# Gated recurrence and binary FFN on one core: the mix difference in another buffer, a step's tanh ahead of a copy, gating in the x tile, and one form for the last rounds

## The chip, the cores and the metric

The kernel runs on one core of one Trainium2 chip. The metric is the device time of one execution in microseconds, lower is better. The time before is 449.11 us, the median of three runs (447.16 to 449.99). A core has five engines with an instruction queue each: PE multiplies matrices, ACT applies functions element by element, DVE and POOL do vector arithmetic, SP issues most DMAs. Each engine works through its queue in order, and semaphores hold an instruction until its inputs are there. Times inside the kernel are from one profiled execution, counted from the start of its span.

## The reference

The input x is 2 sequences of 4096 rows with 256 numbers each.

```python
u = x @ W_in + b_in;  g = sigmoid(x @ W_gate + b_gate)
h_t = tanh(h_prev @ A + u_t @ Bm)              # along the sequence
y_t = g_t * (h_t @ C.T + u_t @ D.T) + (1.0 - g_t) * x_t
x = layernorm(x + (ys @ W_out + b_out + x))
h = gelu(x @ bw1.T + b1, exact)                # 1024 wide, bw = mean(|w|) * sign(w)
x = layernorm(x + (h @ bw2.T + b2))
```

So there are a recurrence with a gate and a residual, a layer norm, a feed-forward layer whose weights are signs with a scale per row, and a second layer norm.

## The kernel before, in words

**Recurrence.** Each sequence is cut into 64 segments of 64 positions; 128 segments advance side by side. A step (`steps`, L157 and L158) is one product of the state tile `st` on PE and one tanh on ACT; each needs the tanh before it. There are 48 warm-up steps that give each segment its start state, and then 64. `compare` and `count` count whether the start states agree with the end states, and a slow path at the end of the kernel, not taken here, redoes the work if they don't.

**Chunks.** The rows are worked on in 16 chunks of 512. For one chunk:

- `gates` (L313) multiplies x by the gate weights on PE, and a tanh on ACT (L365) writes the gate tile `tg`. Early in the kernel this work is cut into pieces (`parts`) that fill PE between steps. Their tanh is passed through `later`, which keeps one back, and the next step releases it.
- `mix` computes C h + D u on PE (L374, `ps_y`), adds the output bias to the chunk's rows `xn` on POOL (L359), and forms the difference `d` to x on DVE (L381). `mix_end` gates it with two DVE operations (L386 and L389), and y is the result.
- `project` multiplies y by W_out (L399, `ps_z`), and DVE adds the rows (L410). `stats1` collects the statistics, with an inverse root on POOL (L266); `shift` (L271, DVE) and `norm` (L279, ACT) apply them.
- The normed rows are then turned. For chunks 0, 1 and 15 `turn` does it on PE (L430). For the others (`far` in the loop) `blocks` transposes 32x32 blocks on DVE (L449), sixteen DMAs on SP's queue put them in place (L455), `split_hi` copies the result to a rounded high part on ACT (L463), and `split_lo` forms the rest on DVE (L467). High and low parts are `xhi` and `xlo`.
- The feed-forward layer has four groups. `up(g)` multiplies by signs on PE (L486, `ps_h`), takes two gelus on ACT (L496) and a rounded high copy (L505). `low(g)` forms the rest on DVE (L512). `down(g)` multiplies both by the second signs (L528, `ps_o`). `down 3` ends with a scaling on DVE (L544, tile `o`).
- `add` (L550) adds the rows, `stats` collects statistics, `store` shifts and norms, on ACT or DVE, and issues the DMA to `out_y` on SP.

**Buffers.** Tiles with one tag share a fixed number of buffers, and an instruction that writes a tile waits until a buffer is free. `ps_h`, `ps_g`, `ps_u` and the product of `count` share three PSUM buffers; `ps_y`, `ps_z` (from chunk 2 on) and `ps_t` share one; `ps_o` has one. Gate tiles have nine, x tiles eight, `xhi` two, and `o` one, shared by the scaled output and by the mix difference.

**Order.** The order is written out by hand. The order in which the Python code calls pieces is the order of each engine's queue. `emit` and `do` add up a cost for pieces and put a step in when a pace is reached; `step()` puts one in directly while any are left. A round c of the main loop (c from 0 to 14) works on `up` of chunk c, the end of chunk c-1, the turning of chunk c+1, and mix and projection of chunk c+2. After round 14 the rest of chunk 15 is written out. Before the loop, chunks 0 to 2 are mixed, projected and normed among the last pieces of gates. `load` gets a chunk's inputs and states (`hu`), `load_n` its rows (`xn`); both queue on SP. A step that completes chunk 0, 1 or 2 issues the load of its states.

Round 14 is written differently from the others before the change: chunk 13's `add` is on POOL, its `stats` stands after `low 2`, and its `store` is on DVE behind `down 1`.

Of the kernel before, what the change touches and what calls it, by code (L numbers as in the profile page):

```python
# [8 lines left out]
FP = mybir.dt.float32  # L9
# [7 lines left out]
P = 128  # L17
B, T, DM, S, H = 2, 4096, 256, 64, 1024
KD = DM // P
# [4 lines left out]
N = 512  # L24
# [3 lines left out]
TB = N // P  # L28
# [9 lines left out]
def gated_recurrence_then_binary_ffn(  # L38
# [16 lines left out]
    nc = tc.nc  # L55
# [227 lines left out]
    def all_stats(r, name):  # L283
# [2 lines left out]
            what(range(TB))  # L286
        return st

    waiting = None

    def later(what, *args):
        if waiting is None:
            what(*args)
        else:
            waiting.append((what, args))
            if len(waiting) > 1:
                what, args = waiting.pop(0)
                what(*args)

# [29 lines left out]
    class Chunk:  # L329


        def __init__(self, c, name, at=lambda a, c: a[c]):
            self.c, self.nm, self.at, self.xt = c, name, at, None
            self.far = False

        def load_x(self):
            self.xt = xp.tile([P, KD, N], FP, tag="xt", name=f"xt_{self.nm}", bufs=XTB)
# [31 lines left out]
        def mix(self):  # L369

            nm, xt_ = self.nm, self.xt
            ps = p_m.tile([P, KD, N], FP, tag="m", name=f"ps_y{nm}")
            for m in range(KD):
                nc.tensor.matmul(  # L374
                    ps[:, m, :], cd[:, bass.ts(m, P)], self.hu, start=True, stop=True
                )
                if m < KD - 1:
                    yield
            self.add_row(self.xn, bo_r)
            self.d = wk.tile([P, KD, N], FP, tag="o", name=f"d{nm}", bufs=1)  # L380
            nc.vector.tensor_sub(self.d, ps, xt_)  # L381
            yield

        def mix_end(self):
            d = self.d
            nc.vector.scalar_tensor_tensor(d, self.t, 1.0, d, ALU.add, ALU.mult)  # L386
            yield
            y = self.y = self.t
            nc.vector.scalar_tensor_tensor(y, self.xt, 2.0, d, ALU.mult, ALU.add)  # L389
            yield  # L390

# [251 lines left out]
    done = 0  # L643
# [6 lines left out]
    def next_steps():  # L650
        nonlocal done
        steps(plan[done])
        done += 1
        if done == WARM:
            first_states()
        for i in range(3):
            if done == WARM + (i + 1) * SPC:
                ch[i].load_h()
        for what, args in waiting or ():
            what(*args)  # L660
        if waiting:
            waiting.clear()

    def emit(what, pieces, pace=5600):
# [8 lines left out]
    def step():  # L673
        if ready():
            next_steps()
# [17 lines left out]
    def parts(n, pace):  # L693
        emit("part", (next(early, None) for _ in range(n)), pace)

    ET = mybir.EngineType
    with tc.manual_schedule(engines={ET.PE, ET.Activation, ET.DVE, ET.Pool, ET.SP}):
        waiting = []
        for c in range(FIRST + 1, FIRST + 6):
            load_xT(c)  # L700
        idle_products(7)
        emit("u", u_of_chunks(FIRST), 1 << 30)
        since = 0
        pairs = [(5, 6), (7, 8), (9, 10), (11, 12), (13, 14), (), (1, 2)]
        loads = [[10, 11], [12, 13], [14, 15, 0], [1, 2], [3], [], []]
        for n, pair in enumerate(pairs):
            before = 2 if n == 0 else 1
            parts(before, EARLY)
            if pair:
                emit("", u_of_chunks(*pair))  # L710
                if pair == (13, 14):
                    emit("", u_of_chunks(15, 0))
                emit("u", [None], EARLY)
            for c in loads[n]:
                load_xT(c)
            if n == 0:
                load_weights()
            if n == 3:
                halve_weights()
            if n >= 5:  # L720
                load_xT(n + 3)
                for i in ((0,), (1, 2))[n - 5]:
                    ch[i].load_n()
                    ch[i].load_u()
            for i in range(7 - before):
                if 1 <= n < 5 and i == 0:
                    load_w(n - 1)
                if 2 <= n < 6 and i == 3:
                    prepare_w(n - 2)
                parts(1 if (n, i) != (6, 5) else 0, EARLY)  # L730
        assert done >= WARM + SPC, done
        emit("u", u_of_chunks(3), EARLY)
        for i in range(4):
            ch[i].xt = x_tiles[i]
        do(0, "mix", pace=850)
        do(0, "mix_end")
        parts(2, 600)
        assert done >= WARM + 2 * SPC, done
        do(1, "mix", pace=850)
        do(1, "mix_end")  # L740
        parts(1, 600)
        do(0, "project", 0, p_2, "o", pace=1700)
        do(0, "project", 1, pace=1700)
        do(0, "stats1")
        assert done >= WARM + 3 * SPC, done
        do(2, "mix", pace=1700)
        do(0, "shift")
        do(1, "project", 0, p_2, "o", pace=1700)
        do(0, "norm")
        do(1, "project", 1, pace=1700)  # L750
        do(1, "stats1")
        mixed = ch[2].mix_end()
        next(mixed)
        parts(1, 1700)
        while waiting:
            next_steps()
        waiting = None
        do(0, "turn", True)
        emit("", mean_w2())
        do(1, "norm", nc.vector)  # L760
        do(0, "rest")
        next(mixed)
        parts(2, 1700)
        for i in (4, 5):
            do(i, "load_x")
        end = len(ch) - 1
        parts_met = compare()
        since = -1 << 40
        late = gates(ch[10:], TB)
        for c in range(end):  # L770
            far = 0 < c < end - 1
            if c > 0:
                do(c + 1, "shift")
                do(c + 1, "norm")
                do(c - 1, "low", 3)
                if far:
                    do(c + 1, "blocks")
            do(c, "up", 0)
            step()
            do(c - 1, "down", 2)  # L780
            if c == end - 2:
                do(c, "low", 0)
            if c > 0:
                do(c + 2, "mix")
                do(c + 2, "mix_end")
            if c != end - 2:
                do(c, "low", 0)
            if c == end - 1:
                next(parts_met)
                next(parts_met)  # L790
            do(c + 3, "load")
            do(c + 6, "load_x")
            if c % 2 == 0:
                do(10 + c // 2, "load_gate_x")
            do(c, "up", 1)
            step()
            do(c - 1, "down", 3)

            def add():
                do(c - 1, "add", range(TB), nc.gpsimd if c == end - 1 else nc.vector)  # L800
                if c < end - 1:
# [8 lines left out]
            if c == end - 1:  # L810
                next(parts_met)
                next(parts_met)
            if not 1 <= c <= 12:
                add()
            do(c + 1, "rest")
            do(c, "up", 2)
            if far:
                do(c + 1, "split_hi")
            do(c, "low", 2)
            if c < end - 1:  # L820
                do(c - 1, "store", range(TB), nc.scalar)
                do(c + 3, "load_n")
            if c == end - 1:
                do(c - 1, "stats")
            if c == end - 2:
                assert done == len(plan), done
# [94 lines left out]
```

## Time and profile before

| what | value |
|---|---|
| median of three runs | 449.11 us (447.16 to 449.99) |
| the profiled execution | 451.14 us |
| its span on the core | 449.4 us |
| mean granted PE clock | 0.994 |
| PE busy | 428.2 us, 95% of the span |
| DVE busy | 332.0 us, 74% |
| ACT busy | 284.4 us, 63% |
| POOL busy | 152.5 us, 34% |

A line of a group or a timeline names the start and duration in us, the engine, the line of the kernel, the operation, what it writes and reads (`out<-in`, shapes, number of instructions), and in brackets the idle time before it with what ended it. A window line gives the busy time and the number of instructions of PE, of PE's weight loads, of DVE, ACT and POOL, then the granted clock as a share of full speed, the DMA engines' share and GB/s. A wait line names the one that waited and the one waited for, with total us, number of times and the longest.

### The profile page before, as it was taken

The numbers are of one execution on the slowest core, as the hardware profiler recorded it, in microseconds if no ns is written. First come the engines' busy times: TensorE is split into PE (matmuls) and PEld (weight loads), VectorE is DVE, ScalarE is ACT, GpSimd is POOL, SyncE is SP. The second block draws the span as 40 slices with busy tenths as digits, with TensorE's granted clock in tenths as the row PEclk, the third lists the DMA queues.
The fourth block names the chain that finished last, engine by engine and source line by source line (L and its number), as shares of the span: only waits on it lengthen the run. The fifth ranks groups of instructions, "written<-read, shape, count | busy, mean of one in ns | idle before, by whom it ended". The sixth has DMA issues, their size and how long they took to land.

```text
span 449.4 us, 6825 instructions
## 1 busy us (share of the span) xinstructions
PE 428.2 (95%) x2402; PEld 344.2 (77%) x2402; DVE 332.0 (74%) x571; ACT 284.4 (63%) x476; POOL 152.5 (34%) x177
## 2 busy tenths in 40 slices
PE   8999998989999999999999999999999999898992
PEld 4665766678887879787878787878787878687882
DVE  0245946786878788887888797869797979795874
ACT  2443441575676666767676777767776776848571
POOL 1000510364042425252525343434343445352513
PEclk9999999999999999999999999999999999999997
DMA  8877523400151615162515242524242223210102
GB/s 292 293 281 257 196 82 123 160 1 0 41 171 42 216 39 175 34 190 68 154 53 185 75 136 69 188 72 141 69 144 69 78 86 86 85 44 28 47 1 99
DMA packets 31480, 51.34 MB, mean 114 GB/s; under 512 B 5329, under 2 KB 19665, under 8 KB 31441
## 3 DMA queue, kind: packets, MB, share of 16 engines
q1 hardware_dynamic: 30864, 50.48, 35.7%
q8 instruction: 21, 0.34, 0.3%
q10 hardware_dynamic: 576, 0.37, 0.3%
q14 instruction: 19, 0.15, 0.1%
HBM read 31.43 MB, written 8.39 MB: 89 GB/s over the span
## 4 chain that ended last, share of the span: by engine, by line
PE 61%; DVE 12%; SPq 9%; ACT 8%; DMA 4%; issue 3%; POOL 2%; POOLq 0%; DVEq 0%; ACTq 0%
PE ps_o L528 15%; PE ps_h L486 14%; PE ps_g L313 10%; SPq L455 9%; PE ps_z L399 8%; PE ps_s L157 5%; PE ps_y L374 5%; ACT xn L279 4%; PE ps_u L131 3%; DVE hlo L512 2%; DMA xt<-in_xT 2%; DMA hu<-st 1%; ACT h L496 1%; DMA xlo<-xb 1%; DVE bs_a L256 1%
## 5 line engine op out<-in xcount | busy, mean ns | idle before, releaser
L528 PE MATMUL ps_o<-sg,hhi 128*128 128x256 f32 x496 | 121.8, 286 | 2.1 <-DVE o L544 2.1
L528 PE MATMUL ps_o<-sg,hlo 128*128 128x256 f32 x496 | 118.3, 279 | 0.8 <-DVE hlo L512 0.8
L496 ACT ACTIVATE h<-ps_h,bias_c,al 128x512 f32<-128x512 f32 x128 | 95.7, 772 | 27.8 <-PE ps_h L486 23.5
L528 PEld LDWEIGHTS ps_o<-sg,hhi 128*128 128x128 f32 x496 | 93.6, 189 | 3.3 <-DVE o L544 2.6
L528 PEld LDWEIGHTS ps_o<-sg,hlo 128*128 128x128 f32 x496 | 93.5, 189 | 2.0 <-DVE hlo L512 1.2
L486 PE MATMUL ps_h<-xhi,sg 128*128 128x512 f32 x256 | 93.0, 444 | 1.4 <-ACT h L496 1.4
L512 DVE TENSOR_TENSOR hlo<-h,hhi 128x1024 fp32r<-128x1024 f32 (+1 forms) x65 | 78.4, 1224 | 6.5 <-ACT hhi L505 6.4
L486 PE MATMUL ps_h<-xlo,sg 128*128 128x512 f32 x256 | 80.1, 393 | 1.3 <-DVE xlo L440 1.2
L359 POOL TENSOR_TENSOR xn<-xn,bo_r 128x256 f32<-128x256 f32 x64 | 50.5, 820 | 82.8 <-DMA xn<-in_x 77.5
L266 POOL TENSOR_TENSOR rs_b<-rs_b,neg_half 128x4 f32<-128x4 f32 (+1 forms) x17 | 28.1, 1655 | 120.9 <-DVE rs_b L265 120.8
L505 ACT CAST hhi<-h 128x1024 fp32r<-128x1024 f32 (+1 forms) x65 | 67.4, 1038 | 2.0
L313 PE MATMUL ps_g<-xt,w_gate 128*128 128x384 f32 (+3 forms) x208 | 66.2, 430 | 0.1
L486 PEld LDWEIGHTS ps_h<-xhi,sg 128*128 128x128 f32 x256 | 46.5, 189 | 20.0 <-issue 11.7
L157 PEld LDWEIGHTS ps_s<-st,wab 128*128 128x128 f32 x224 | 37.9, 189 | 27.7 <-ACT st L158 16.0
L158 ACT ACTIVATE st<-ps_s 64x128 f32<-64x128 f32 x112 | 30.0, 268 | 45.7 <-PE ps_s L157 45.3
L399 PE MATMUL ps_z<-w_out,tg 128*128 128x256 f32 x256 | 58.2, 379 | 0.0
L486 PEld LDWEIGHTS ps_h<-xlo,sg 128*128 128x128 f32 x256 | 48.1, 188 | 12.8 <-DVE xlo L440 2.1
L359 POOL TENSOR_TENSOR xn<-xn,b_r 128x256 f32<-128x256 f32 x64 | 51.3, 831 | 2.0 <-PE ps_t L430 2.0
L399 PEld LDWEIGHTS ps_z<-w_out,tg 128*128 128x128 f32 x256 | 47.2, 190 | 5.7
L157 PE MATMUL ps_s<-st,wab 128*128 128x128 f32 x224 | 44.6, 281 | 3.7 <-ACT st L158 3.5
L266 POOL TENSOR_TENSOR rs_a<-rs_a,neg_half 128x4 f32<-128x4 f32 x16 | 17.2, 1076 | 72.5 <-DVE rs_a L265 69.3
L279 ACT ACTIVATE xn<-xn,nm_a,rs_a 128x256 f32<-128x256 f32 x60 | 31.2, 591 | 14.6 <-DVE nm_a L271 14.6
(76 smaller groups left out, 466.5 us busy)
## 6 DMA issues: line engine op xcount, KB each, us to landing
xt<-in_xT SPq DMA_DIRECT2D x35, 512.0 KB, 4.3
xn<-in_x SPq DMA_DIRECT2D x16, 512.0 KB, 3.3
out_y<-xn SPq DMA_DIRECT2D x15, 512.0 KB, 2.6
xlo<-xb SPq DMA_DIRECT2D x208, 32.0 KB, 1.9
hu<-st SPq DMA_DIRECT2D x32, 128.0 KB, 2.3
w1t<-in_w1T SPq DMA_DIRECT2D x2, 512.0 KB, 5.1
w1n<-in_w SPq DMA_DIRECT2D x2, 512.0 KB, 6.3
w2t<-in_w2T SPq DMA_DIRECT2D x2, 512.0 KB, 5.3
```

The lines of the kernel that those rows point to most:

```text
L157: nc.tensor.matmul(p_h, ab, st[:, j].rearrange("p b k -> p (b k)"), start=True, stop=True)
L266: nc.gpsimd.tensor_tensor(rs, rs, neg_half[:, cut], ALU.pow)
L279: nc.scalar.activation(r, r, AF.Identity, bias=self.sh[:, i : i + 1], scale=rs)
L313: nc.tensor.matmul(ps[:, cut], w_gate[:, k, bass.ts(m, P)], xt_[:, k, cut], start=k == 0 and i == 0, stop=k == KD - 1, skip_group_check=True,)
L359: nc.gpsimd.tensor_tensor(r[:, i, :], r[:, i, :], row, ALU.add)
L399: nc.tensor.matmul(self.ps_z[:, i, :], self.y[:, k, bass.ts(i, P)], w_out[:, k, :], start=k == 0, stop=k == KD - 1,)
L455: nc.sync.dma_start(out=self.lo.bitcast(FP)[bass.ts(q, 32), :, bass.ts(a, P)], in_=xb[bass.ts(a, 32), q :: Q, :, :].rearrange("p k i c -> ...
L486: nc.tensor.matmul(ps, sg1[:, k, bass.ts(j, P)], part[:, k, :], start=n == 0, stop=n == 2 * KD - 1,)
L496: nc.scalar.activation(to, ps.rearrange("p (a i c) -> p a i c", a=P // 32, c=32) if self.far else ps, AF.Gelu, bias=b1_c[:, j : j + 1], sc ...
L505: nc.scalar.copy(hi[:, part, :], h[:, part, :])
L512: nc.vector.tensor_sub(lo[:, i, :], h[:, i, :], hi[:, i, :].bitcast(FP))
L528: nc.tensor.matmul(ps[:, i, :], part[:, j % 2, bass.ts(tb, P)], sg2[:, j, :], start=j == 0 and part is self.h[j // 2][0] and first, stop=j ...
```

## The change

- The mix difference `d` takes one of the two `xhi` buffers; `o` is left to the scaled output.
- For chunks 0 and 1 (`in_x`) y is written to the x tile instead of the gate tile.
- Before the loop, one piece of gates stands ahead of chunk 0's mix instead of behind chunk 1's. While `held` is set, `later` and the steps don't release tanhs. The first gating of chunk 2 stands behind chunk 0's turn. The rows of chunk 1 are loaded first, and those of chunks 2 and 0 ahead of the inputs `hu` of chunks 1 and 2.
- In a round, `low 0` stands between the mix difference and the first gating, and the second gating behind the scaling in `down 3`. The third step stands ahead of `split_hi` and of the store instead of behind them.
- Round 14 takes the order of the others: `add` on DVE, `stats` behind it, `store` on ACT ahead of `up 3`. Only `up 0` now stands ahead of chunk 15's norm and chunk 13's `low 3`.

```diff
-            if len(waiting) > 1:
+            if len(waiting) > 1 and not held:
...
-            self.d = wk.tile([P, KD, N], FP, tag="o", name=f"d{nm}", bufs=1)
+            self.d = wk.tile([P, KD, N], FP, tag="xhi", name=f"d{nm}")
...
-            y = self.y = self.t
+            y = self.y = self.xt if self.in_x else self.t
...
-        for what, args in waiting or ():
-            what(*args)
-        if waiting:
+        if waiting and not held:
+            for what, args in waiting:
+                what(*args)
             waiting.clear()
...
-                for i in ((0,), (1, 2))[n - 5]:
-                    ch[i].load_n()
-                    ch[i].load_u()
+                ch[n - 4].load_n()
+                if n == 5:
+                    ch[0].load_u()
+                else:
+                    ch[0].load_n()
+                    ch[1].load_u()
+                    ch[2].load_u()
...
+        ch[0].in_x = ch[1].in_x = True
+        parts(1, 600)
         do(0, "mix", pace=850)
         do(0, "mix_end")
+        held = True
         parts(2, 600)
         assert done >= WARM + 2 * SPC, done
         do(1, "mix", pace=850)
         do(1, "mix_end")
-        parts(1, 600)
+        held = False
...
-        mixed = ch[2].mix_end()
-        next(mixed)
         parts(1, 1700)
...
         emit("", mean_w2())
+        mixed = ch[2].mix_end()
+        next(mixed)
...
-            if c > 0:
+            if far:
                 do(c + 1, "shift")
                 do(c + 1, "norm")
                 do(c - 1, "low", 3)
-                if far:
-                    do(c + 1, "blocks")
+                do(c + 1, "blocks")
             do(c, "up", 0)
+            if c == end - 1:
+                do(c - 1, "low", 3)
+                do(c + 1, "shift")
+                do(c + 1, "norm")
             step()
             do(c - 1, "down", 2)
-            if c == end - 2:
-                do(c, "low", 0)
             if c > 0:
                 do(c + 2, "mix")
-                do(c + 2, "mix_end")
-            if c != end - 2:
-                do(c, "low", 0)
+            do(c, "low", 0)
+            mixed = ch[c + 2].mix_end() if 0 < c < end - 1 else iter(())
+            next(mixed, None)
...
             do(c - 1, "down", 3)
+            next(mixed, None)
...
-                do(c - 1, "add", range(TB), nc.gpsimd if c == end - 1 else nc.vector)
-                if c < end - 1:
-                    do(c - 1, "stats")
+                do(c - 1, "add")
+                do(c - 1, "stats")
...
             do(c, "up", 2)
+            step()
             if far:
                 do(c + 1, "split_hi")
             do(c, "low", 2)
-            if c < end - 1:
-                do(c - 1, "store", range(TB), nc.scalar)
-                do(c + 3, "load_n")
-            if c == end - 1:
-                do(c - 1, "stats")
...
-            step()
+            do(c - 1, "store", range(TB), nc.scalar)
+            do(c + 3, "load_n")
             do(c, "down", 0)
...
-            if c == end - 1:
-                do(c - 1, "store")
```

More of the change, by code (lines that the diff above doesn't have):

```diff
@@ L333, in __init__ @@
             self.c, self.nm, self.at, self.xt = c, name, at, None
-            self.far = False
+            self.far = self.in_x = False
         def load_x(self):
@@ L740, in gated_recurrence_then_binary_ffn @@
         do(1, "mix_end")
-        parts(1, 600)
+        held = False
         do(0, "project", 0, p_2, "o", pace=1700)
@@ L775, in gated_recurrence_then_binary_ffn @@
                 do(c - 1, "low", 3)
-                if far:
-                    do(c + 1, "blocks")
+                do(c + 1, "blocks")
             do(c, "up", 0)
+            if c == end - 1:
+                do(c - 1, "low", 3)
+                do(c + 1, "shift")
+                do(c + 1, "norm")
             step()
             do(c - 1, "down", 2)
-            if c == end - 2:
-                do(c, "low", 0)
             if c > 0:
                 do(c + 2, "mix")
-                do(c + 2, "mix_end")
-            if c != end - 2:
-                do(c, "low", 0)
+            do(c, "low", 0)
+            mixed = ch[c + 2].mix_end() if 0 < c < end - 1 else iter(())
+            next(mixed, None)
             if c == end - 1:
+                assert done == len(plan), done
                 next(parts_met)
@@ L810, in gated_recurrence_then_binary_ffn @@
             if c == end - 1:
+                assert done == len(plan), done
                 next(parts_met)
@@ L819, in gated_recurrence_then_binary_ffn @@
             do(c, "low", 2)
-            if c < end - 1:
-                do(c - 1, "store", range(TB), nc.scalar)
-                do(c + 3, "load_n")
-            if c == end - 1:
-                do(c - 1, "stats")
-            if c == end - 2:
-                assert done == len(plan), done
-            step()
+            do(c - 1, "store", range(TB), nc.scalar)
+            do(c + 3, "load_n")
             do(c, "down", 0)
```

## The prediction

> **What bounds the kernel now.** I read the page first, then the waits, then the matmul engine's timeline around each hole, then a table of windows cut at the ends of the projections (one window is one round of the main loop).
>
> ```profile
> span 449.4 us, 6825 instructions
> PE 428.2 (95%) x2402; PEld 344.2 (77%) x2402; DVE 332.0 (74%) x571; ACT 284.4 (63%) x476; POOL 152.5 (34%) x177
> ```
>
> PE is the bound: it has work for 428.2 of 449.4 us, and the change adds or drops no matmul. So only PE's holes can be won: 3.4 us in the start (70.8 to 91.5), 2.7 in the main loop, 4.35 at the end (391 to 438). The last 8.6 us, after PE's last product at 440.84, is a chain that stays. The holes by their releasers, from the waits:
>
> ```profile
> PE ps_s L157 <- ACT st L158: 3.5, 6, 0.9
> PE ps_o L528 <- DVE o L544: 2.1, 1, 2.1
> PE ps_h L486 <- ACT h L496: 1.4, 1, 1.4
> PE ps_h L486 <- DVE xlo L440: 1.2, 1, 1.2
> PE ps_y L374 <- DMA hu<-st: 1.2, 1, 1.2
> PE ps_o L528 <- DVE hlo L512: 0.8, 1, 0.8
> ```
>
> The columns are total us, times, longest. The first is mostly the main loop's; ACT's timeline shows where it comes from:
>
> ```profile
> 236.70 1.05 ACT L505 CAST hhi<-h 128x1024 fp32r<-128x1024 f32 x1
> 240.45 1.05 ACT L463 CAST xhi<-xlo 128x1024 fp32r<-128x1024 f32 x1 [2.70 <-DMA xlo<-xb]
> 241.41 2.08 ACT L279 ACTIVATE xn<-xn,nm_b,rs_b 128x256 f32<-128x256 f32 x4
> 243.39 0.25 ACT L158 ACTIVATE st<-ps_s 64x128 f32<-64x128 f32 x1
> ```
>
> The step's tanh (L158) has had its product since about 236.1. It stands behind the high copy, which waits for the transposed blocks, and four norms. PE's next step product starts at 243.69 after a hole of 0.49.
>
> **Middle: the step ahead of the high copy.** The step issues one product, one tanh and, in these rounds, no DMA. On PE it keeps its place (behind `up 2`, ahead of `down 0`); on ACT it passes one cast and four norms; SP and POOL are not touched. The tanh then runs near 237.8, six us before it is needed. What is won, from the windows (start and end of a round, its length):
>
> ```profile
> 126.29:149.71 23.42, 22.85 (x129) 18.80 (x129) 18.55 (x32) 16.51 (x27) 8.27 (x11) 1.00 0.40 111
> 172.99:195.50 22.51, 22.51 (x130) 18.84 (x129) 18.55 (x32) 15.74 (x26) 8.64 (x11) 1.00 0.33 99
> 287.49:311.01 23.52, 22.87 (x130) 18.82 (x129) 18.55 (x32) 17.58 (x29) 8.61 (x11) 1.00 0.46 140
> ```
>
> The nine rounds from 126.29 to 333.61 take 207.3; a round without a hole takes 22.51 to 22.63, so nine take 203.2: 4.1. The holes alone sum to 2.7 [...]. I take 3.8, because blocks arrive late in some rounds; ends 2.7 and 4.1. Next in line is the following step, which needs a tanh done at 246.22 and stands at 247.68; with PE 0.65 earlier and that tanh 0.25 earlier, 1.1 remains.
>
> The other edits of a round cost nothing. `low 0` moves ahead of both gatings and the scaling between them; they stay the same DVE instructions of 1.2 each, and y is ready near 258 against a projection at 261. The difference in `xhi`: the high copy takes the difference's old buffer, which DVE frees near 258, 2.5 before the blocks land; the difference takes the buffer that `up 3` of the round before has left. If the first cover were gone, the copy would wait for `up 3`, some 2 us later a round; nothing in the order asks for that.
>
> **Start.** Three holes. (1) PE waits 1.15 for chunk 1's states: their load is issued at 68.33 and lands at 71.84. A piece (0.65) and its step (0.22) now stand ahead of chunk 0's mix, so that load is released one step earlier relative to mix 1: issue near 67.9, landing near 71.4, PE there at 71.3. Residue 0.1. Chunk 0's mix comes 0.87 later for it; its y ends on DVE near 73.2, and its projection starts at 73.7. (2) Tanh of chunk 9 waits 3.41 on ACT for the projection of chunk 0, whose y lies in the gate buffer it needs, and holds a step (hole 0.93). With y in x that buffer is free after the first gating (near 72), and the held tanh is issued later still: gone. (3) PE waits 1.23 for chunk 0's low part. Everything is 2.3 earlier by then, and chunk 2's first gating (1.22) now follows the low part. But transposes of chunk 1 wait for DVE's norm, with the same DVE work ahead: 94.37 less 2.3 is 92.05, against PE's 95.41 now. Total 3.3; ends 2.0 (the load as late as PE waits for it, (3) only shifted) and 3.5. The reordered loads take chunks 2 and 0's rows out from behind SP's wait for chunk 1's inputs (61.24): they land near 55 and their row additions end long before 77. x tiles live a few us longer; eight buffers cover it.
>
> **End: round 13.** DVE, from the mix's end at 386.3: difference 1.22, low 1.66, gating 1.23, scaling 1.23 gives 391.7; PE wants it at 391.9, so the 2.15 hole closes. Then gating 1.22, low 1.22, add 1.22, statistics 1.94, POOL's root 1.86, shift 0.70: 399.9 instead of 400.9. From there x1 and the low part of chunk 14 end at 402.5, not 403.36, and PE, at 400.75, waits for it. So 2.3 shrinks to 1.0.
>
> **End: round 14, where the change adds a wait.** The store of chunk 13 returns to ACT, ahead of `up 3`'s gelus, and its shift needs statistics that now stand on DVE behind lo(15), low 1, two compares and the add. ACT: norm(12) 399.9 to 402.0; gelus 1.43, cast 1.05; gelus 1.43, cast 1.05: 406.9; norm(15) 2.08, gelus 1.45, cast 1.05, xhi(15) 1.01: 412.4. DVE: lo 1.23, low 1.22, compares 1.04, add 1.22, statistics 1.94: 419.1. POOL's root: 1.02 with DVE idle, 1.86 beside a low (both rows in the trace); a low is beside it: 421.0. Shift 0.17 to 0.70: 421.5. ACT then norms 2.08 and gives the first gelu 0.78 later, 424.4. Queued behind that norm are all of chunk 14's last gelus and chunk 15's first; PE waits for them, since `up` of chunk 15 needs one of three ps_h buffers. PE is there at 417.8 (404.0 plus six groups of 1.85, 0.85 of transposes and `down 1` 1.85). Hole 6.6; it starts at 424.4 what starts at 420.66 today: +3.7. No row shows this wait; unless the statistics come 4 us earlier it can't vanish, and each us of POOL or DVE moves it by one.
>
> **A rule against the change.** Row first:
>
> ```profile
> 443.00:444.00 1.00, 0.00 (x0) 0.00 (x0) 0.28 (x2) 0.36 (x1) 0.60 (x1) 1.00 0.25 86
> 444.00:445.00 1.00, 0.00 (x0) 0.00 (x0) 0.73 (x2) 0.00 (x0) 0.09 (x1) 0.59 0.53 176
> 445.00:446.00 1.00, 0.00 (x0) 0.00 (x0) 0.00 (x0) 0.00 (x0) 0.00 (x0) 0.50 0.62 199
> ```
>
> ```profile
> 1.00 3.18 PE L154 MATMUL ps_s<-ones 128*128 128x128 f32 x14 [1.00 <-POOL ones L107]
> ```
>
> In the windows the third column from the end is the granted clock: it halves near 444.2, 3.3 us after PE's last product. And in the timeline the kernel's first fourteen products run 0.21 us apart, about twice the 0.11 that L157's take later. [...] None of today's holes is that long; a 6.6 us hole is. Restart at half pace for about 3.5 us, as at the start (row: 1.0 to 4.2 and a little beyond), costs 1.7. Without the rule the end is +2.4, with it +4.1: `up` of 15 to 428.0, two groups of 1.85 to 431.7, against 427.57 today, the two later holes of 0.8 included. I take 4.1; ends -2 and +5.5.
>
> **Sum.** -3.3 - 3.8 + 4.1 = -3.0. The profiled execution took 451.14 (span 449.4 and 1.7 around it): 448.1 after. It lies 2.0 above the median of the runs, 449.11; on that, 446.1.
>
> **Rivals.**
> - *The hole is there, but the clock holds* [...]: -3.3 - 3.8 + 2.4, 444.4. For it: another buffer could be freed by the flag's copy, at 421.9, for a hole of 4.
> - *Round 14 gains too*: the statistics come in time, and of the 4.35 of holes 2 is won: -9.1, 440.0. For it: today's 1.37 hole (norm ahead of the gelus) is really removed, DVE loses the store's 1.38. Against it: the ACT chain above has no idle time to give.
> - *The blocks set the round* (the other side): low part, statistics, norm, block transpose, sixteen DMAs of 0.64, high copy is a ring through four engines. Its turn from 219.90 to 241.50 is 21.6; others 21.0 to 22.4. If it comes to 23.0, the mean of today's nine rounds, PE's freed time turns into a wait for the low part: middle 0, and -3.3 + 4.1 = +0.8, 449.9, slower. Against: rounds of 22.5 exist. It decides from a turn of 22.6 on.
> - That the change does not do what it says: a tanh placed ahead still waits only if its product is late; L157 is behind `up 2` and was done by 236.1.
>
> **Chances.** Forecast 0.48 (446.1, give or take 1.6), clock holds 0.17, round 14 gains 0.25, ring 0.10. A bound of 1% (4.5 us) is about what a measurement of this kernel tells from no change: faster than 444.6 are the third case, 0.25, two thirds of the second, 0.11, and a sixth of the first, 0.08; slower than 453.6 only the ring with the end at its worst, 0.04. Range: 439.6 leaves out a third of the third case, 448.6 the ring and a sliver of the first; together 0.2.
>
> **What would show it.** No wait of L157 on L158 over 0.1 us after 100 us; rounds of 22.5 to 22.6; chunk 2's mix near 77.5 and the first chunk 0 lo product near 87.7; no hole before chunk 13's `down 0`; then one hole of 5 to 7 us before chunk 15's `up 0`, ACT idle until nm_b, granted clock 0.5 behind it. Wrong if that hole is under 3 us, or if rounds stay at 23.

## The result and the profile after

The changed kernel takes 445.02 us, the median of five runs (444.3 to 445.99); the kernel before took 449.07 in five runs beside it (447.16 to 449.99). The ratio is 0.9918, with a 95% interval of 0.9889 to 0.9946. The forecast was 446.1, in a range of 439.6 to 448.6.

The profiled execution took 445.99 us. These are the span and the busy times of its page:

```profile
span 444.1 us, 6819 instructions
PE 428.2 (96%) x2402; PEld 346.8 (78%) x2402; DVE 332.6 (75%) x569; ACT 285.5 (64%) x480; POOL 153.3 (35%) x176
```

PE has the same 2402 matmuls; the span is 5.3 us shorter. That its busy time is 428.2 us in both is chance, as the stages below show. The waits of PE (total us, times, longest) show where holes went and came:

```profile
PE ps_h L487 <- DVE flag L178: 2.9, 1, 2.9
PE ps_h L487 <- ACT h L497: 1.5, 1, 1.5
...
PE ps_h L487 <- DVE xlo L468: 0.8, 1, 0.8
```

The line of a step that waits for its tanh (3.5 us in six waits), `o`'s 2.1, chunk 0's low part and the states' load are gone. What is left of over 0.2 us behind the kernel's first products stands at the end, and most of it in one place that the kernel before didn't have, ahead of chunk 15's `up 0`. From here on, the line numbers of the changed kernel are one higher than before from the mix on (`up` is L487, the gelu L497, the high copy of `h` L506).

**The sum by stage.** The stages are cut at the ends of projections (L399 before, L400 after) on PE:

| stage | before | after | difference |
|---|---|---|---|
| start to the end of chunk 2's projection | 103.78 | 99.63 | -4.15 |
| from there to chunk 14's projection (twelve rounds) | 273.43 | 268.67 | -4.76 |
| round 13, to chunk 15's projection | 22.38 | 20.01 | -2.37 |
| from there to PE's last product | 41.25 | 47.05 | +5.80 |
| behind it, and around the span | 10.30 | 10.63 | +0.33 |

The sum is -5.15, the difference of the two profiled executions. The medians are 4.05 apart: the profiled execution of before lies 2.0 above its median, and the experiments show that most of this is in its start. PE's busy time falls by 0.37, 2.09 and 0.22 us in the first three stages (in the twelve rounds because a round with a hole also keeps PE busy longer, 22.85 against 22.51 in the prediction's windows) and rises by 2.70 in the fourth, where the clock falls (below).

**Middle.** In the main loop the high copy still waits for its blocks, but nothing that PE needs stands behind it. ACT's timeline of the changed kernel (start, duration, then the operation). The bracket of the high copy names a DVE operation that ended at 233.34; the last of the copy's blocks landed at 233.66:

```profile
230.02 1.05 ACT L506 CAST hhi<-h 128x1024 fp32r<-128x1024 f32 x1
230.97 0.26 ACT L158 ACTIVATE st<-ps_s 64x128 f32<-64x128 f32 x1
233.88 1.05 ACT L464 CAST xhi<-xlo 128x1024 fp32r<-128x1024 f32 x1 [2.64 <-DVE hlo L513]
234.83 2.08 ACT L279 ACTIVATE xn<-xn,nm_b,rs_b 128x256 f32<-128x256 f32 x4
```

The tanh of the step (L158) now runs ahead of the copy's 2.64 of waiting, not behind four norms. Windows cut at the projections (start and end, length; busy time and count of PE, weight loads, DVE, ACT, POOL; granted clock; DMA share; GB/s) show what that does to a round:

```profile
122.14:144.65 22.51, 22.51 (x130) 18.84 (x129) 18.45 (x32) 16.03 (x27) 8.29 (x11) 1.00 0.35 105
279.69:302.19 22.50, 22.50 (x129) 18.83 (x129) 19.48 (x32) 17.03 (x27) 9.98 (x10) 1.00 0.46 143
302.19:324.70 22.51, 22.51 (x130) 18.84 (x129) 18.55 (x32) 17.27 (x28) 10.37 (x12) 1.00 0.35 103
```

The length of each round is PE's busy time in it: no hole. Before, most rounds were 22.5 to 22.9 and 23.2 to 23.5 in turn.

**End.** ACT's timeline of the changed kernel, around the store of chunk 13:

```profile
404.41 1.06 ACT L506 CAST hhi<-h 128x1024 fp32r<-128x1024 f32 x1
411.65 2.08 ACT L279 ACTIVATE xn<-xn,nm_b,rs_b 128x256 f32<-128x256 f32 x4 [6.18 <-DVE nm_b L271]
413.63 1.42 ACT L497 ACTIVATE h<-ps_h,bias_c,al 128x512 f32<-128x512 f32 x2
```

ACT stands still for 6.18 us in front of the norm of chunk 13, whose shift comes from DVE at 411.62. DVE's timeline shows the work in front of that shift:

```profile
403.06 1.23 DVE L441 TENSOR_TENSOR xlo<-ps_t,xhi 128x1024 fp32r<-128x1024 f32 x1 [1.32 <-ACT xhi L439]
...
407.02 1.41 DVE L256 BATCH_NORM_STATS2 bs_b<-xn 128x6 f32<-128x256 f32 x4
...
410.94 0.68 DVE L271 SCALAR_TENSOR_TENSOR nm_b<-mv_b,rs_b 128x4 f32<-128x4 f32 x1 [0.90 <-POOL rs_b L266]
...
411.54 0.14 DVE L178 CAST flag<-ps_cnt 1x1 int32<-1x1 f32 x1
```

And PE's timeline in the same stretch:

```profile
408.62 0.19 PE L177 MATMUL ps_cnt<-cnt,ones 128*1 128x1 f32 x2
411.73 0.73 PE L487 MATMUL ps_h<-xhi,sg 128*128 128x512 f32 x2 [2.92 <-DVE flag L178]
412.30 0.63 PE L487 MATMUL ps_h<-xlo,sg 128*128 128x512 f32 x2
414.44 1.22 PE L487 MATMUL ps_h<-xhi,sg 128*128 128x512 f32 x2 [1.51 <-ACT h L497]
415.46 1.05 PE L487 MATMUL ps_h<-xlo,sg 128*128 128x512 f32 x2
```

Two holes, 2.92 and 1.51, with 1.2 us of work between them. The products of L487 behind the second are slower: 1.22 and 1.05 for a pair that took 0.73 and 0.63 just before. Windows over this stretch give the clock, in the third column from the end:

```profile
411.73:413.68 1.95, 1.20 (x4) 0.67 (x4) 0.00 (x0) 1.95 (x5) 1.94 (x3) 1.00 0.00 0
413.68:420.51 6.83, 6.07 (x24) 5.68 (x25) 2.45 (x2) 4.81 (x7) 0.00 (x0) 0.50 0.19 77
```

The clock falls to half at 413.68 and stays there for 6.83 us.

### The profile page after: what moved, and what is told of

Same layout as the page of the kernel before. It is cut to its first block, busy times and chain, and to the rows that moved or that the text cites. A ratio compares the mean times of both kernels' runs of the same rounds, so it can differ in the third digit from the quotient of the medians.

```text
span 444.1 us, 6819 instructions
## 1 busy us (share of the span) xinstructions
PE 428.2 (96%) x2402; PEld 346.8 (78%) x2402; DVE 332.6 (75%) x569; ACT 285.5 (64%) x480; POOL 153.3 (35%) x176
## 4 chain that ended last, share of the span: by engine, by line
PE 84%; DVE 6%; ACT 4%; DMA 1%; POOL 1%; issue 1%; SPq 0%; POOLq 0%; DVEq 0%
PE ps_h L487 23%; PE ps_o L529 23%; PE ps_g L314 12%; PE ps_z L400 11%; PE ps_y L375 6%; PE ps_s L157 6%; PE ps_u L131 3%; ACT xn L279 2%; DMA xt<-in_xT 1%; ACT h L497 1%; DVE hlo L513 1%; POOL rs_b L266 1%; DVE bs_b L256 1%; ACT hhi L506 1%; DVE xlo L441 1%
## 5 line engine op out<-in xcount | busy, mean ns | idle before, releaser
L529 PE MATMUL ps_o<-sg,hhi 128*128 128x256 f32 x496 | 123.2, 288 | 0.0
L529 PE MATMUL ps_o<-sg,hlo 128*128 128x256 f32 x496 | 119.6, 281 | 0.1
L497 ACT ACTIVATE h<-ps_h,bias_c,al 128x512 f32<-128x512 f32 x128 | 95.2, 771 | 19.4 <-PE ps_h L487 16.1
L487 PE MATMUL ps_h<-xhi,sg 128*128 128x512 f32 x256 | 93.4, 446 | 4.4 <-DVE flag L178 2.9
L529 PEld LDWEIGHTS ps_o<-sg,hhi 128*128 128x128 f32 x496 | 95.0, 192 | 1.0 <-DVE o L545 0.2
L529 PEld LDWEIGHTS ps_o<-sg,hlo 128*128 128x128 f32 x496 | 94.8, 191 | 1.1 <-DVE hlo L513 0.3
L513 DVE TENSOR_TENSOR hlo<-h,hhi 128x1024 fp32r<-128x1024 f32 (+1 forms) x65 | 80.2, 1251 | 9.0 <-ACT hhi L506 9.0
L360 POOL TENSOR_TENSOR xn<-xn,bo_r 128x256 f32<-128x256 f32 x64 | 52.8, 856 | 90.2 <-DMA xn<-in_x 78.7
L487 PE MATMUL ps_h<-xlo,sg 128*128 128x512 f32 x256 | 80.5, 395 | 0.9 <-DVE xlo L468 0.8
L506 ACT CAST hhi<-h 128x1024 fp32r<-128x1024 f32 (+1 forms) x65 | 67.4, 1039 | 2.0
L487 PEld LDWEIGHTS ps_h<-xhi,sg 128*128 128x128 f32 x256 | 46.6, 190 | 23.1 <-issue 11.7
L158 ACT ACTIVATE st<-ps_s 64x128 f32<-64x128 f32 x112 | 29.9, 267 | 45.9 <-PE ps_s L157 45.5
L487 PEld LDWEIGHTS ps_h<-xlo,sg 128*128 128x128 f32 x256 | 48.3, 189 | 12.7 <-DVE xlo L468 1.2
L157 PEld LDWEIGHTS ps_s<-st,wab 128*128 128x128 f32 x224 | 38.5, 189 | 21.6 <-ACT st L158 9.6
L360 POOL TENSOR_TENSOR xn<-xn,b_r 128x256 f32<-128x256 f32 x64 | 52.3, 848 | 1.1 <-PE ps_t L431 1.1
L400 PE MATMUL ps_z<-w_out,tg 128*128 128x256 f32 x224 | 50.6, 379 | 0.0
L400 PEld LDWEIGHTS ps_z<-w_out,tg 128*128 128x128 f32 x224 | 41.4, 190 | 5.1
L157 PE MATMUL ps_s<-st,wab 128*128 128x128 f32 x224 | 43.8, 277 | 0.1
L279 ACT ACTIVATE xn<-xn,nm_b,rs_b 128x256 f32<-128x256 f32 x62 | 32.3, 591 | 10.4 <-DVE nm_b L271 10.4
```

What stands on the lines that cost most here:

```text
L157: nc.tensor.matmul(p_h, ab, st[:, j].rearrange("p b k -> p (b k)"), start=True, stop=True)
L158: nc.scalar.activation(h_of[:, j + 1].rearrange("p b k -> p (b k)"), p_h[TOP, :], AF.Tanh)
L279: nc.scalar.activation(r, r, AF.Identity, bias=self.sh[:, i : i + 1], scale=rs)
L360: nc.gpsimd.tensor_tensor(r[:, i, :], r[:, i, :], row, ALU.add)
L400: nc.tensor.matmul(self.ps_z[:, i, :], self.y[:, k, bass.ts(i, P)], w_out[:, k, :], start=k == 0, stop=k == KD - 1,)
L487: nc.tensor.matmul(ps, sg1[:, k, bass.ts(j, P)], part[:, k, :], start=n == 0, stop=n == 2 * KD - 1,)
```

## The experiments

The theory: each of the parts does what the prediction says, and round 14's new form gives a good part of the gain back. Rivals to it: the loop is bound by its ring of blocks and the gain there is chance; only the store on ACT is bad in round 14, or all of its new form; the half clock costs nothing beside the hole. Each kernel was timed beside the kernel before on the same chip (449.69, 449.55 and 450.15 us, the medians of three batches). The changed kernel was run again in the second batch; differences from it are taken to this median, and come out about 0.2 us smaller for kernels of the first batch if the ratios are compared instead. What was expected of this run:

> The changed kernel once more, beside the parts of the change and in the same job. As before: about 0.992 of the kernel before, holes of 2.9 and 1.5 us ahead of chunk 15's up 0, half clock behind them.

It took 445.35 us, ratio 0.9894 (0.9872 to 0.9916), with the same holes of 2.86 and 1.52. The result and its place repeat.

### The step's tanh alone

The kernel before, with only the third step of a round moved:

```diff
             do(c, "up", 2)
+            step()
             if far:
                 do(c + 1, "split_hi")
...
-            step()
             do(c, "down", 0)
```

> The kernel before with one edit: in every round the third step stands behind up 2, ahead of the high copy and the store. My theory (the tanh stood behind the high copy and the four norms): rounds 3 to 10 all take 22.5 to 22.6 us, no wait of L157 on L158 over 0.1 us in the main loop, and the time falls by 4 us, to about 445.1. Rival (the ring through the block DMAs sets the round): the rounds keep alternating between 22.5 and 23.4 us, the hole moves to the first low product of up 0, and the time falls by less than 1 us.

It took 445.37 us, ratio 0.9901 (0.9872 to 0.9929): 4.3 us won by moving one call. Windows cut at the projections, as above:

```profile
102.17:124.67 22.50, 22.50 (x129) 18.83 (x129) 18.05 (x31) 14.73 (x23) 8.53 (x9) 1.00 0.16 35
124.67:147.18 22.51, 22.51 (x129) 18.84 (x129) 18.56 (x32) 16.10 (x26) 8.27 (x11) 1.00 0.35 105
...
282.47:304.98 22.51, 22.51 (x129) 18.84 (x129) 19.84 (x32) 16.67 (x27) 10.04 (x10) 1.00 0.44 133
```

All rounds are without a hole (one takes 22.76, all of it busy), and the ring of blocks doesn't bind: with PE's holes gone, it keeps up with 22.5. The waits of PE in this kernel also show which holes this edit leaves:

```profile
PE ps_o L528 <- DVE o L544: 2.1, 1, 2.1
PE ps_h L486 <- ACT h L496: 1.4, 1, 1.4
PE ps_h L486 <- DVE xlo L440: 1.2, 1, 1.2
...
PE ps_s L157 <- ACT st L158: 0.9, 1, 0.9
...
PE ps_y L374 <- DMA hu<-st: 0.3, 1, 0.3
```

The one remaining wait of L157 is the start's. The last line matters for the start, since it is another wait than the 1.15 of before. It stands at the mix of chunk 0, not of chunk 1:

```profile
66.31 1.10 PE L374 MATMUL ps_y<-hu,cd 128*128 128x512 f32 x2 [0.27 <-DMA hu<-st]
```

Chunk 1's states, whose load took 3.51 from issue to landing in the profile of before, took 2.19 here and in the kernel that has the round's order alone (below), with the same code there, and PE doesn't wait for them at all; in that kernel, too, the wait, 0.37, is for chunk 0's states.

### The start alone

The changed kernel with its main loop, round 14 and the buffer of the difference as before, so that only the edits ahead of the loop remain (a piece of gates ahead of chunk 0's mix, `held`, y in x, chunk 2's first gating, the order of loads).

> The kernel before with the edits ahead of the main loop alone: order of the loads, one piece of gates ahead of chunk 0's mix, held tanhs, y of chunks 0 and 1 in x, chunk 2's gating behind chunk 0's turn. My theory: the three holes of the start close (in the run with the step alone they were 0.27, 0.93 and 1.24), chunk 2's projection ends near 99.7 as in the changed kernel, and the time falls by 2.8 us, to 446.7. Rival (a round of the main loop absorbs the earlier start, since the block DMAs come no earlier): less than 1 us.

It took 447.49 us, ratio 0.9945 (0.9924 to 0.9966): 2.1 won. Chunk 2's projection ends at 99.46, as in the changed kernel (99.63) and 2.5 to 2.7 earlier than in the two kernels with the old start (102.17 and 101.94). So beside these two executions the start brings some 2.3 to 2.7, and some of it is lost in the loop, whose rounds still alternate between 22.5 and 23.6 with waits of up to 0.84 for a tanh.

Which edit closes the first hole and which the third (chunk 0's low part) was not taken apart. For the second, two experiments take one of the start's edits away from the changed kernel. First y in the gate tile again:

```diff
-        ch[0].in_x = ch[1].in_x = True
```

> The changed kernel with y of chunks 0 and 1 in the gate tiles again; the held tanhs stay. My theory (the gate buffer is what chunk 9's tanh waits for): that tanh waits on ACT for chunk 0's projection again, and a hole of about 0.9 us on PE comes back near 75; 1 us slower than the changed kernel. Rival (holding the tanh back until the projection is enough by itself): no hole and no difference.

It took 445.06 us, ratio 0.9897 (0.9874 to 0.992), the time of the changed kernel. ACT's timeline shows that the tanh of a gate does wait there:

```profile
75.36 0.27 ACT L158 ACTIVATE st<-ps_s 64x128 f32<-64x128 f32 x1 [1.71 <-PE ps_s L157]
77.09 0.69 ACT L366 ACTIVATE tg<-ps_g,bg_c 128x512 f32<-128x512 f32 x1 [1.46 <-PE ps_z L400]
77.68 0.26 ACT L158 ACTIVATE st<-ps_s 64x128 f32<-64x128 f32 x1
```

It waits 1.46 for the projection (L400) that reads the gate tile, and the step's tanh behind it ends at 77.94. PE's product of the next step starts at 78.83 and isn't held. The expected hole of 0.9 did not come back: holding the tanh back is enough. Then the other way, y in x but nothing held:

```diff
-        held = True
```

> The changed kernel with y of chunks 0 and 1 in x, but without the holding back of tanhs. With the run that had the holding alone this asks which of the two edits closes the hole ahead of chunk 2's mix. If either is enough: chunk 9's tanh is issued ahead of chunk 1's mix, waits for nothing since chunk 0's first gating has freed the buffer, no hole, and the time of the changed kernel within 0.5 us. If only the holding does it: a hole near 71 to 77 of 0.5 us or more, and as much slower.

It took 445.53 us, ratio 0.9897 (0.9878 to 0.9915). The tanh waits 0.34, for chunk 0's first gating, and PE has no hole:

```profile
71.22 0.69 ACT L366 ACTIVATE tg<-ps_g,bg_c 128x512 f32<-128x512 f32 x1 [0.34 <-DVE d L387]
```

Either edit alone closes this hole. The kernel without both was not tried: a step would then stand behind a tanh that waits for a projection behind that step.

### The round's order and the difference's buffer alone

The kernel before with the difference in `xhi`, `low 0` ahead of both gatings in every round, and the second gating behind `down 3`:

```diff
-            self.d = wk.tile([P, KD, N], FP, tag="o", name=f"d{nm}", bufs=1)
+            self.d = wk.tile([P, KD, N], FP, tag="xhi", name=f"d{nm}")
...
-            if c == end - 2:
-                do(c, "low", 0)
             if c > 0:
                 do(c + 2, "mix")
-                do(c + 2, "mix_end")
-            if c != end - 2:
-                do(c, "low", 0)
+            do(c, "low", 0)
+            mixed = ch[c + 2].mix_end() if 0 < c < end - 1 else iter(())
+            next(mixed, None)
...
+            next(mixed, None)
```

> The kernel before with the mix difference in the xhi buffers, low 0 behind the difference and the second gating behind the scaling, in all rounds; steps, start and round 14 as before. My theory: rounds 2 to 12 unchanged (22.5 to 23.5), the hole of 2.1 us ahead of round 13's down 0 closes and about 0.8 us of it comes back as a wait for chunk 14's low part: 1.3 us faster, 448.4. Rival (the high copy waits for the buffer it now shares with the difference): a new wait of the high copy on DVE or PE, 1 us or more a round, over 455.

It took 448.66 us, ratio 0.9977 (0.9964 to 0.9989): 0.9 won, and all of it at the end. Windows of an early round and of round 13:

```profile
124.44:148.04 23.60, 22.86 (x129) 18.81 (x129) 18.39 (x32) 16.80 (x28) 8.28 (x11) 1.00 0.38 110
375.25:395.21 19.96, 19.96 (x118) 17.19 (x117) 17.60 (x32) 14.77 (x21) 9.15 (x10) 1.00 0.31 87
```

Early rounds are what they were. Round 13 loses its hole of 2.1 and is 19.96 instead of 22.38; 0.72 comes back as a wait for chunk 14's low part (0.79 in the changed kernel). No wait for a buffer of `xhi` appears: the high copies start at most 0.33 us after the last of their blocks has landed, against 0.31 in the kernel before. The sum of the three kernels with one part each is -4.3 - 2.1 - 0.9 = -7.3. All three parts together are the next kernel, which wins 8.3; the 1.0 beyond the sum is within what the intervals of the three leave open.

### Round 14 as before

The changed kernel with round 14 in its old form:

```diff
-            if far:
+            if c > 0:
                 do(c + 1, "shift")
...
             do(c, "up", 0)
-            if c == end - 1:
-                do(c - 1, "low", 3)
-                do(c + 1, "shift")
-                do(c + 1, "norm")
...
-                do(c - 1, "add")
-                do(c - 1, "stats")
+                do(c - 1, "add", range(TB), nc.gpsimd if c == end - 1 else nc.vector)
+                if c < end - 1:
+                    do(c - 1, "stats")
...
-            do(c - 1, "store", range(TB), nc.scalar)
-            do(c + 3, "load_n")
+            if c < end - 1:
+                do(c - 1, "store", range(TB), nc.scalar)
+                do(c + 3, "load_n")
+            else:
+                do(c - 1, "stats")
...
             do(c, "down", 1)
+            if c == end - 1:
+                do(c - 1, "store")
```

> The changed kernel with round 14 as it was before: chunk 15's norm and chunk 13's low 3 ahead of up 0, chunk 13's add on POOL, its stats behind low 2, its store on DVE behind down 1. My theory (the new round 14 holds ACT for 6.2 us, opens holes of 2.9 and 1.5 us on PE and then runs it at half clock): no hole over 2 us, no half clock before the end, and a time about 5 us under the changed kernel, 440. Rival (the last rounds are bound by PE's work and the holes are only where the slack shows): within 1 us of the changed kernel, 445.

It took 441.4 us, ratio 0.9809 (0.9781 to 0.9838), 8.3 under the kernel before and 4.0 under the changed one (445.35); from chunk 15's projection to the last product the profiles are 4.80 apart (42.25 against 47.05). Its holes at the end are 0.75, 1.47 and 0.80, and the granted clock doesn't fall. So the changed form of round 14 costs 4.0 us.

### The hole filled with products that compute nothing

How much of that is the clock? The changed kernel with 26 idle products (13 pairs of 128x128 into the step's PSUM tile, whose result nobody reads) behind the count:

```diff
         count()
+        idle_products(13)
         do(end, "up", 0)
```

> The changed kernel with 13 products of ones that nobody reads (2.8 us) between the count and chunk 15's up 0, in PE's hole of 2.9 us. It adds work and takes no wait away. My theory (half of the loss at the end is the half clock that follows the hole): the granted clock stays at 1.00, the 32 products of down 2 and down 3 take 3.7 us instead of 5.8, and the time falls by 3 us, to 442. Rival (the half clock follows from something else, or costs nothing since ACT and DVE are late there anyway): the time stays within 0.5 us of the changed kernel or rises.

It took 443.36 us, ratio 0.9855 (0.9826 to 0.9883), 2.0 under the changed kernel. PE's timeline of this kernel:

```profile
409.02 0.19 PE L177 MATMUL ps_cnt<-cnt,ones 128*1 128x1 f32 x2
409.14 3.17 PE L154 MATMUL ps_s<-ones 128*128 128x128 f32 x26
412.17 0.74 PE L487 MATMUL ps_h<-xhi,sg 128*128 128x512 f32 x2
...
414.88 0.73 PE L487 MATMUL ps_h<-xhi,sg 128*128 128x512 f32 x2 [1.52 <-ACT h L497]
```

The first group starts 0.4 later than in the changed kernel, the second hole is the same 1.52, and yet the pair behind it takes 0.73, not 1.22. The windows give the clock:

```profile
412.00:413.00 1.00, 1.00 (x7) 0.79 (x6) 0.12 (x2) 0.91 (x2) 1.00 (x3) 1.00 0.00 0
413.00:414.00 1.00, 0.36 (x2) 0.00 (x0) 0.00 (x0) 1.00 (x3) 1.00 (x2) 1.00 0.00 0
414.00:416.00 2.00, 1.11 (x5) 0.94 (x6) 0.00 (x0) 1.97 (x4) 0.11 (x1) 1.00 0.49 199
416.00:418.00 2.00, 2.00 (x19) 1.92 (x18) 1.23 (x1) 1.97 (x4) 0.00 (x0) 1.00 0.16 64
418.00:420.00 2.00, 2.00 (x18) 1.96 (x18) 0.96 (x1) 1.01 (x1) 0.00 (x0) 1.00 0.03 8
```

It is 1.00 all through. So in this kernel the half clock comes with the 2.92 us of idle time ahead, and it costs some 2.0 us by the medians; from chunk 15's projection to the last product the two profiled executions are 2.7 apart (44.3 against 47.05). That leaves about 2.0 of round 14's 4.0 for the holes themselves.

One hole is enough for it. In the kernel with y in the gate tile again (above), the clock is at half from the end of the first hole, before the second one of 0.68; PE's timeline and a window:

```profile
412.07 1.18 PE L487 MATMUL ps_h<-xhi,sg 128*128 128x512 f32 x2 [2.88 <-DVE flag L178]
```

```profile
412.14:418.97 6.83, 6.15 (x19) 4.85 (x20) 1.27 (x2) 6.69 (x10) 1.87 (x3) 0.50 0.19 77
```

### Chunk 13's store behind what PE waits for

If the norm at the head of ACT's queue is the cause, everything else of the new round can stay:

```diff
-            do(c - 1, "store", range(TB), nc.scalar)
+            if c < end - 1:
+                do(c - 1, "store", range(TB), nc.scalar)
             do(c + 3, "load_n")
...
         do(end - 1, "low", 3)
+        do(end - 2, "store", range(TB), nc.scalar)
         do(end, "low", 0)
```

> The changed kernel with one instruction group moved: chunk 13's store (a shift on DVE, four norms on ACT, a DMA) stands behind chunk 15's up 0 and chunk 14's low 3 instead of ahead of chunk 14's up 3. My theory (the norms, in order ahead of the last gelus, are all of the loss at the end): both holes and the half clock go, PE reaches the end of down 3 near 414.5 instead of 422.1, and the time falls by 7 us, to 438, under both kernels. Rival (the statistics are late, and the norms hold ACT wherever they stand): the hole moves to down 2 or down 3 of chunk 14 and less than 3 us are won.

It took 438.09 us, ratio 0.9737 (0.9709 to 0.9766): 7.3 under the changed kernel, 3.3 under the one with the old round 14, and faster than both the kernel before and the changed one. PE's timeline:

```profile
408.78 0.19 PE L177 MATMUL ps_cnt<-cnt,ones 128*1 128x1 f32 x2
408.90 0.74 PE L487 MATMUL ps_h<-xhi,sg 128*128 128x512 f32 x2
```

`up 0` of chunk 15 follows the count at once. ACT's timeline:

```profile
410.34 1.50 ACT L497 ACTIVATE h<-ps_h,bias_c,al 128x512 f32<-128x512 f32 x2 [1.41 <-DVE flag L178]
411.87 1.05 ACT L506 CAST hhi<-h 128x1024 fp32r<-128x1024 f32 x1
412.83 2.08 ACT L279 ACTIVATE xn<-xn,nm_b,rs_b 128x256 f32<-128x256 f32 x4
```

The norm runs at 412.83, with its shift done at 412.08, and PE has no hole there. Behind the projection of chunk 15, PE's holes are 0.78 and 0.08. So the fault is not the new form of round 14 as a whole, which is better than the old one by 3.3 us (its holes of 1.47 and 0.80 are gone); it is the place of one store. The shift on DVE and the norms on ACT were moved together; that the norms are the part that counts is read from the changed kernel's trace, where ACT's last gelus stand behind them.

### Chunk 12's store too

The hole of 0.78 that remains is the wait for chunk 14's low part, which on DVE stands behind the shift of chunk 12's store and its wait of 0.91 for POOL's root. As above, and in round 13 the store of chunk 12 behind `up 3`:

```diff
-            if c < end - 1:
+            if c < end - 2:
                 do(c - 1, "store", range(TB), nc.scalar)
...
+            if c == end - 2:
+                do(c - 1, "store", range(TB), nc.scalar)
             step()
```

> The kernel with chunk 13's store moved (run e4), and in round 13 chunk 12's store behind up 3 as well, so that DVE forms chunk 15's rows and chunk 14's low part without waiting 0.9 us for POOL's root and the shift. Theory: the last hole of the loop (0.78 us ahead of the first low products of round 14) closes and the time falls by 0.7 us under e4, to 437.4. Rival: the high copy of chunk 14 (ended 390.6 there) then bounds that low part, or the moved norms hold the gelus of round 14, and nothing is won.

It took 438.45 us, ratio 0.9744 (0.9723 to 0.9764): the same time as without it, against the 437.4 expected. The hole of 0.78 is down to 0.08, but PE's timeline has two new ones:

```profile
397.12 0.73 PE L487 MATMUL ps_h<-xhi,sg 128*128 128x512 f32 x2 [0.24 <-ACT h L497]
...
400.85 0.76 PE L431 MATMUL ps_t<-ident,xn 128*128 128x128 f32 x5 [0.16 <-ACT xn L279]
```

The moved norm now stands in front of gelus that PE needs next, and of chunk 15's norm, and from there to the end of chunk 15's high copy (394.32 to 404.11) ACT has no idle time. So in this stretch ACT is short of time; another order of the same work was not tried.

## Why the prediction was right, point by point

- **Middle: the step ahead of the high copy** was right, -3.8. The step alone won 4.3, a little over the upper end of 4.1, and in the two profiles this stretch is 4.76 shorter: 2.67 of holes and 2.09 of PE's busy time. Beyond the holes the upper end counts 1.4, and PE's busy time fell by more than that: rounds come down to 22.51, at the low edge of "22.5 to 22.6". What keeps PE busy longer in a round with a hole is not shown.
- **The other edits of a round cost nothing** was right for rounds 1 to 12: with these edits alone they still alternate between 22.5 and 23.6, and there is no wait for a buffer.
- **Start** was right in its mechanism and mis-sized in term (1). The three holes are gone, and chunk 2's mix and chunk 0's first low product are at 76.89 and 86.71 (77.5 and 87.7 were named). But the load's 1.15 was a late one of that execution: it took 3.51 to land, and 2.19 in two others with the same code, where PE doesn't wait for chunk 1's states but 0.27 and 0.37 for chunk 0's. A sum of 0.3 + 0.9 + 1.2 gives 2.4, what two profiles with the old start show, instead of 3.3; alone the start won 2.1. This lateness is also 0.8 to 0.9 of the 2.0 by which the profiled execution of before lay above its median. For term (2) the prediction gave two reasons, a free buffer and a tanh held back; each is enough without the other.
- **End: round 13** was right: the hole of 2.15 closes, and a wait for chunk 14's low part comes back, 0.79 where 1.3 was forecast. Alone, with the round's other edits, it is worth 0.9; forecast 1.0.
- **End: round 14, where the change adds a wait** was right about the wait and mis-sized in the hole. ACT is idle until `nm_b`, as forecast. But the step said that PE stands for 6.6 us until the second norm and a gelu free a `ps_h` buffer. There was another buffer, the count's, which the flag's copy frees right behind `nm_b`: the first group took it at 411.73, after 2.92, and only the second waited for the gelu, 1.51. Without it the hole would have been 5.63 (from 408.81, the end of the count, to 414.44) by an estimate from these lines, since the shift came 2.8 behind PE and not 3.7. By the prediction's own sign, "Wrong if that hole is under 3 us", the step failed, if narrowly. The prediction had this buffer in a rival, and should have had it in the sum: the count is PE's instruction just ahead of `up 0`, and shares its three buffers.
- **A rule against the change**: the clock did fall, and its term was 1.7 against about 2.0 measured with the hole filled. The size is near for partly wrong reasons, and in part by luck: the hole forecast at 6.6 us is 2.92, and the half clock lasted 6.83 us, not 3.5. The step's rows show the clock halving 3.3 us after PE's last product; that a hole between products does the same was the author's estimate, which no row of the kernel before shows. The runs do: here holes of 2.92 and 2.88 us were enough.
- **The end in sum** was +4.1 by the prediction. In the traces it is +3.43 from chunk 14's projection to the last product (-2.37 in round 13, +5.80 behind it); round 14's form alone costs 4.0 by the medians and 4.80 in the traces, where the same steps give 5.1.
- **Rivals.** "The hole is there, but the clock holds" was right in the buffer and wrong in the clock; the kernel with the filled hole is what it describes, 443.36. "The blocks set the round" fell with the step alone. "Round 14 gains too" fell for this change, since the statistics did not come in time; the reason given against it, an ACT chain without idle time, is not what the trace shows, where ACT stands idle for 6.18. With chunk 13's store behind `up 0` the new form does gain, 438.09.

The errors offset one another: about 0.9 too much for the start against 0.5 too little in the middle and some 1 too much loss at the end. The total of 446.1 for a measured 445.0 is therefore as close as it is in part by luck.

## What to carry to other kernels

In an engine that works in order, look at what stands behind each instruction whose input comes late, and put it behind those that the bound engine needs next; a step here, and one store at the end, were worth 4.3 and 7.3 us with no instruction added or dropped; in the 7.3, about 2 are the half clock that went with the holes. An order that suits the middle rounds has to be looked at again in the last ones, where less work lies in front of the late input. When a hole is forecast, go through all buffers of the waiting tile's tag, with the last reader of each: the one that comes free first ends it.

## What had not been expected of the hardware

- The granted clock fell to 0.50 with no hole over 2.92 us: 1.95 us behind the end of that hole in the changed kernel, with PE busy for 1.20 of them, and 0.07 behind the end of a hole of 2.88 in the kernel with y in the gate tile again. It stayed there for 6.83 us, although PE was busy for 6.07 of them in the first and 6.15 in the second. With the first hole filled by 3.17 us of idle products it stayed at 1.00, behind a hole of 1.52. The four traces whose clock falls in the last rounds (the changed kernel twice, y in the gate tile again, nothing held) each have a hole of 2.9 there; the longest hole behind which the clock held is 2.15, in the kernel before. What decides the fall is not separated here.
- At half clock the pairs of L487 took 1.22 and 1.05, against 0.73 and 0.63.
- The load of chunk 1's states took 2.19 us from issue to landing in two executions and 3.51 in a third with the same code in front of it, where it held PE for 1.15. The cause stays open.
